# A Mamba image block: the next step's pieces at other units, and three products for GpSimd

## The chip, the cores and the metric

The kernel runs on one core of a Trainium2 chip. The metric is the device time of one execution in microseconds (us), lower is better. The engines are TensorE (PE, with its weight loads as PEld), VectorE (DVE), ScalarE (ACT), GpSimd (POOL) and SyncE (SP), which here issues every DMA. Each works off its own queue of instructions, and semaphores tie them together.

## The reference

The input is a batch of two images with 96 channels and 128 x 128 pixels. After a layer norm over the channels, four Mamba blocks each read the 16384 pixels as a sequence: by rows, by rows backward, by columns, by columns backward. The part in which the kernel spends most of its time is this (cut from the reference):

```python
xz = x @ in_w.T
xc, z = jnp.split(xz, 2, axis=-1)              # 192 inner channels each
xc = silu(causal_conv4(xc) + conv_b)           # depthwise, 4 taps
dt_raw, Bm, Cm = split(xc @ xproj_w.T)         # 6, 16 and 16 columns
dt = softplus(dt_raw @ dt_w.T + dt_b)
A = -jnp.exp(A_log)                            # 192 x 16
def step(h, t):                                # over the 16384 positions
    dA = jnp.exp(dt_t[:, :, None] * A)
    h = dA * h + dt_t[:, :, None] * B_t[:, None, :] * u_t[:, :, None]
    y = jnp.einsum('bds,bs->bd', h, C_t)
y = (y + Dp * xc) * silu(z)
return y @ outp_w.T
```

The four results are brought back to the order of the image, joined by a 1 x 1 product (`fuse_w`) and added to the input. Then come a feed-forward layer in a reduced float format, a 3 x 3 convolution and a second feed-forward layer, each with a norm ahead of it and a sum behind it.

## The kernel before

Each image goes through three stages: `normalize` (layer norm, and both orders of the pixels written to DRAM), `mamba`, and `ffn_and_conv`. Only `mamba` is touched by the change.

**Steps.** Two sequences are worked at once: first both forward ones, then both backward ones (`PAIRS`). Together they have 384 inner channels, which is three groups `g` of 128 partitions; group 0 belongs to the first sequence, group 2 to the second, group 1 is half and half. A step is 512 positions of both sequences. There are 32 steps for each pair, 64 per image, 128 in all.

**Units.** A step has 24 units (`nu`): group 0, 1 and 2 in turn, and for each the 16 states in pairs. Unit u is group u // 8, states 2 (u mod 8) and the next. Two units share a quad of four states, so a quad starts at every even unit. The step's own work, unit by unit, is:

- SP fetches a B tile and a C tile per quad from DRAM (`row_tile`, 128 x 4 x 512, 1 MB as written), B six units ahead of use and C four units ahead. There are four buffers for B and three for C. A fetch stands in SP's queue until the last reader of its buffer is done, and all later DMAs stand behind it.
- GpSimd multiplies a quad's B tile by dt times xc (`b_part`) and adds the state that enters the step to its first column (the fix, L347).
- ACT computes the decay exp(dt A) for the unit's two states into PSUM (`decay`, two units ahead), and copies the last column of each finished unit for the next step (`hst`, L446).
- VectorE runs one scan per state (`scan`, L357), and one product of both states with C (L445). For the units in `BY_POOL` the scan writes into the B tile in SBUF instead of the decay in PSUM, and GpSimd makes the product (`by_pool`, L364) a unit later.
- PE sums the products over the states in one PSUM bank y, by matmuls with the identity (`sums`, L361). A product by GpSimd is summed two units after its turn.
- At the first unit of a group VectorE multiplies the finished y by silu(z) (`gated`, L368), and PE opens the next y with D times xc (L452). After a group, `project` and `collect` add its share to the image.

**The loop.** Every engine's order is written out by hand (`in_order`), so what the loop issues first stands first in an engine's queue. One iteration k of it is:

```python
if k % 2 == 0:
    fetch(k + 2 * B_AHEAD, 0, B_AHEAD, bs)
    feed(k + AHEAD)                     # b_part
issue(k, 0)
... scan(0, ...); behind(k - 1); feed_decay(k + AHEAD); scan(1, ...)
if k % 2 == 0:
    fetch(k + 2 * C_AHEAD, 1, C_AHEAD, cs)
issue(k, 1)
```

`behind(k - 1)` holds the product, the hst copy and the sums of the unit before. `issue(k, where)` issues pieces that were put at that unit by `later`: where = 0 ahead of the scans, where = 1 at the end of the iteration.

**The next step's pieces.** While a step runs, the next one is prepared in pieces, whose units stand in a list in `prologue` as (unit, where, function). A unit from 24 on falls into the step itself, a negative one into the step before the one in which most of the pieces lie. The pieces are: `load` (two DMAs, tiles xa and xb), `conv` for each group (PE) with `conv_out` (ACT), `mix` (two DMAs that sort group 1's rows) and `silu` (ACT, with a table load before and one after); `rows` (PE: dt_raw, B and C of all positions), `rows_out` (ACT) and `rows_to_dram` (a DMA); `gate` (PE, the z half) with `gate_out` (ACT). For each group there is a chain for dt: `dt_in` (PE), `dt_exp` and `dt_ln` (three ACT instructions each), `dt_q`, `dt_log`, `dt_sum`, `dt_u` (GpSimd). `entry` (ACT) and `entering` (GpSimd) carry the state into the step. conv, rows, gate, dt_in and project all write to one PSUM tile, misc, which has a single buffer: each waits until ACT has read the one before.

Of the kernel before, what the change touches and what calls it, by code (L numbers as in the profile page):

```python
# [32 lines left out]
B_AHEAD = 3  # L33
C_AHEAD = 2
AHEAD = 2
BY_POOL = ((0, 4), (1, 4))
BCO = 32
NBC = 4 * S

# [2 lines left out]
def tile_metaformer(ctx: ExitStack, tc: tile.TileContext, a: dict, out: bass.AP):  # L42
# [136 lines left out]
    def mamba(acc, xnr, xnc):  # L179

        with ExitStack() as st:
# [25 lines left out]
            def prologue(pi, i, d):  # L207
# [107 lines left out]


                first = pi == 0 and i == 0
                at = [(-2, 1, load), (2, 1, partial(mix, "xc")), (6, 1, partial(silu, "xc"))]
                at += [(13, 1, partial(mix, "sz")), (28 if first else 22, 1, partial(silu, "sz"))]
                at += [(9, 0, rows), (10, 0, rows_out), (10, 1, rows_to_dram)]  # L320
                for g, k in ((1, 1), (0, 3), (2, 5)):
                    at += [(k, 0, partial(conv, g)), (k + 1, 0, partial(conv_out, g))]
                for g, k in ((1, 12), (0, 17), (2, 20)):
                    at += [(k, 0, partial(gate, g)), (k + 1, 0, partial(gate_out, g))]
                dts = ((24, 25, 26, 27), (31, 32, 33, 34)) if first else ((14, 15, 16, 18), (19, 20, 21, 23))
                for g, ks in enumerate(((10, 11, 12, 14), *dts)):
                    at += [(k, 0, partial(f, g)) for k, f in zip(ks, (dt_in, dt_exp, dt_ln, dt_q))]
                    at += [(ks[3] + m, 0, partial(f, g)) for m, f in ((1, dt_log), (1, dt_sum), (2, dt_u))]
                    if i > 0:
                        at += [((17, 23, 27)[g], 0, partial(entry, g)), (20 + 8 * g, 1, partial(entering, g))]  # L330

                outs = (conv_out, gate_out, rows_out, dt_exp)
                return sorted(at, key=lambda p: (p[0], p[1], getattr(p[2], "func", p[2]) not in outs))

            def row_tile(d, g, s, k, ahead):

# [19 lines left out]
            def scan(j, da, b, h):  # L356
                nc.vector.tensor_tensor_scan(h[:, j, :], da[:, j, :], b[:, j, :], 0.0, ALU.mult, ALU.add)  # L357

            def sums(s, y, c):
                for j in range(2):  # L360
                    nc.tensor.matmul(y, ident, c[:, j, :], start=False, stop=s + j == S - 1)  # L361
# [4 lines left out]
            def gated(pi, d, g, y):  # L366
                t = d["sz"][:, g, :]
                nc.vector.tensor_tensor(t, y, t, ALU.mult)  # L368
                d["yg"].append(t[:, ::-1] if pi == 1 else t)
# [17 lines left out]
            steps = [(pi, i) for pi in range(2) for i in range(NT)]  # L387
            units = [(g, s) for g in range(NG) for s in range(0, S, 2)]
            nu = len(units)
            total = nu * len(steps)  # L390
            state = [{} for _ in steps]
            todo = {}

            def later(k, where, f, *args):
                todo.setdefault((k, where), []).append(partial(f, *args))

            def issue(k, where):
                for f in todo.pop((k, where), ()):
                    f()

            for k, where, f in prologue(*steps[0], state[0]):
                if k < nu:
                    f()
                else:
                    later(k - nu, where, f)

            def prepare(n):
                if n < len(steps):
                    for m, where, f in prologue(*steps[n], state[n]):
                        k = (n - 1) * nu + m  # L410
                        if k < 0:
                            f()
                        else:
                            later(k, where, f)

            prepare(1)
            bs, cs, das, hs, quads = {}, {}, {}, {}, {}

            def fetch(k, n, ahead, m):
                if k < total:  # L420
                    t = row_tile(state[k // nu], *units[k % nu], n, ahead)
                    m[k], m[k + 1] = t[:, 0:2, :], t[:, 2:4, :]
                    if n == 0:
                        quads[k] = t

            def feed(k):

                if k < total:
                    n = k // nu
                    b_part(steps[n][1], state[n], *units[k % nu], quads.pop(k))  # L430

            def feed_decay(k):
                if k < total:
                    n = k // nu
                    das[k] = decay(steps[n][0], state[n], *units[k % nu])
# [3 lines left out]
            def behind(k):  # L439

                n, u = divmod(k, nu)
                (pi, i), d, (g, s) = steps[n], state[n], units[u]
                h, c = hs.pop(k), cs.pop(k)
                if (g, s) not in BY_POOL:
                    nc.vector.tensor_tensor(c, h, c, ALU.mult)  # L445
                nc.scalar.copy(hst[:, g, s : s + 2], h[:, :, T - 1])  # L446
                if s == 0:
                    if k > 0:
                        pn, pu = divmod(k - 1, nu)
                        gated(steps[pn][0], state[pn], units[pu][0], ys.pop(k - 1))  # L450
                    y = ps_y.tile([128, T], F32, name="y")
                    nc.tensor.matmul(y, dmat[:, pi, g, :], d["xc"][:, g, :], start=True, stop=False)  # L452
                else:
                    y = ys.pop(k - 1)
                ys[k] = y
                if (g, s) in BY_POOL:
                    later(k + 1, 1, by_pool, h, c)
                    later(k + 3, 1, sums, s, y, c)
                else:
                    sums(s, y, c)  # L460
                if k == total - 1:
                    gated(pi, d, g, y)
                if s == S - 2 and g > 0:
                    later(k + 3, 0, project, pi, i, d, g)
                    later(k + 3, 1, collect, pi, d, g)

            for m, (n, ahead) in ((bs, (0, B_AHEAD)), (cs, (1, C_AHEAD))):
                for k in range(ahead):
# [3 lines left out]
                feed_decay(k)  # L472
            for k in range(total + 6):
                n, u = divmod(k, nu)
                if u == nu - 2:

                    prepare(n + 2)
                if k % 2 == 0:
                    fetch(k + 2 * B_AHEAD, 0, B_AHEAD, bs)
                    feed(k + AHEAD)  # L480
                issue(k, 0)
                if k < total:
                    (g, s) = units[u]
                    da, b = das.pop(k), bs.pop(k)
                    hs[k] = b if (g, s) in BY_POOL else da
                    scan(0, da, b, hs[k])
                if 0 < k <= total:
                    behind(k - 1)
                feed_decay(k + AHEAD)
                if k < total:  # L490
                    scan(1, da, b, hs[k])
# [3 lines that stand above are left out]
# [102 lines left out]
    for b in range(NB):  # L597
        xnr = dpool.tile([C, L], F32, name="xnr")
        xnc = dpool.tile([C, L], F32, name="xnc")
        normalize(b, acc, xnr, xnc)  # L600
        mamba(acc, xnr, xnc)
        ffn_and_conv(b, acc)
# [71 lines left out]
```

## Time and profile before

| what | us |
|---|---|
| median of 3 runs | 12153.81 (12136.48 to 12159.19) |
| the profiled execution's own time | 12198.56 |
| its span, first to last instruction | 12196.8 |
| Mamba stage of the first image, 151.4 to 5532.9 | 5381.5 |
| Mamba stage of the second image, 6234.8 to 11618.2 | 5383.4 |
| VectorE busy in the first of these | 5177.9 |
| GpSimd busy in the first of these | 4869.7 |
| ACT busy in the first of these | 3888.1 |

The two Mamba stages are 88% of the span, so the time is mostly that of 128 steps. In the profile a group of instructions is a line of the kernel on one engine. Its row tells the busy time, the mean length of one instruction in ns, and after the bar the idle time of its engine just before it, with what ended most of that. An instruction's own length overlaps with its neighbour's a little on VectorE and ACT; where a chain is added up, the distance from one start to the next is the better measure. All B and C tiles carry the name row, the scan's result the name da, or row where it is written into the B tile.

### The profile page before, as it was taken

To read this page: it belongs to the slowest core of one execution; us is meant where nothing else is said; L and a number is where in the kernel's file an instruction comes from. 1 tells how busy PE (TensorE), PEld (TensorE's weight loads), DVE (VectorE), ACT (ScalarE), POOL (GpSimd) and SP (SyncE) were. 2 spreads that over 40 slices of the span, in tenths; PEclk is the share of its full clock that TensorE was granted. 3 is DMA by queue.
4 is the path that set the end of the run, shared out by engine and by line. 5 is a ranking of instruction groups with operands and counts; after the bars stand their busy time and mean duration, and the time that the engine had idled before them with its cause. 6 is when DMAs were issued, how large, how long until landed. Compare 5 with 4: busy or idle time off the path is not lost. (4 is left out here: it accounts for less than half of the span.)

```text
span 12196.8 us, 95712 instructions
## 1 busy us (share of the span) xinstructions
PE 10601.0 (87%) x24208; PEld 4012.8 (33%) x24208; DVE 10962.5 (90%) x10624; ACT 8585.5 (70%) x15110; POOL 9908.7 (81%) x5336
## 2 busy tenths in 40 slices
PE   7888888888888888888978888888888888888889
PEld 2333333333333333333323333333333333333333
DVE  6999999999999999995469999999999999999954
ACT  6777777777777777775577777777777777777655
POOL 5998999999998989891159989999989999988811
PEclk9999999999999999999989999999999999999999
DMA  7887888788877878781068888888878878878700
GB/s 250 309 319 302 307 319 313 309 318 312 318 310 306 319 305 310 308 317 47 26 242 307 308 317 312 314 318 313 313 307 308 321 308 316 314 305 309 304 32 13
DMA packets 539169, 3417.07 MB, mean 280 GB/s; under 512 B 67276, under 2 KB 68396, under 8 KB 140696
## 3 DMA queue, kind: packets, MB, share of 16 engines
q1 hardware_dynamic: 538616, 3410.94, 72.9%
q8 instruction: 195, 3.19, 0.1%
q14 instruction: 358, 2.93, 0.1%
HBM read 3289.04 MB, written 54.53 MB: 274 GB/s over the span
## 5 line engine op out<-in xcount | busy, mean ns | idle before, releaser
L345 POOL TENSOR_TENSOR row<-dtu,row 128x2048 f32<-128x2048 f32 x1536 | 6949.9, 4525 | 820.8 <-DMA row<-bcd 658.5
L357 DVE TENSOR_TENSOR_SCAN da<-da,row 128x512 f32<-128x512 f32 x5632 | 6650.2, 1215 | 509.8 <-ACT da L353 187.3
L361 PE MATMUL y<-row,ident 128*128 128x512 f32 x12288 | 5957.9, 618 | 1130.5 <-DVE row L445 1125.7
L353 ACT ACTIVATE da<-dt,amat 128x512 f32<-128x512 f32 x6144 | 4250.4, 692 | 278.7 <-DVE row L357 92.0
L361 PEld LDWEIGHTS y<-row,ident 128*128 128x128 f32 x12288 | 2268.5, 194 | 4643.0 <-issue 2296.4
L445 DVE TENSOR_TENSOR row<-da,row 128x1024 f32<-128x1024 f32 x2816 | 3395.8, 1206 | 1.0 <-DMA row<-bcd 0.9
L446 ACT COPY hst<-da 128x2 f32<-128x2 f32 x2816 | 434.7, 154 | 1423.8 <-DVE row L445 1412.4
L204 PE MATMUL misc<-xa,inx 96*64 96x512 f32 (+1 forms) x2048 | 963.6, 614 | 131.3 <-DMA xa<-xnr 108.0
L204 PE MATMUL misc<-xb,inx 96*64 96x512 f32 (+1 forms) x2048 | 962.3, 613 | 1.9 <-ACT xc L231 1.6
L568 POOL TENSOR_TENSOR acc<-acc,y 96x512 f32<-96x512 f32 x128 | 147.4, 1152 | 987.1 <-DVE y L567 987.1
L357 DVE TENSOR_TENSOR_SCAN row<-da,row 128x512 f32<-128x512 f32 x512 | 616.9, 1205 | 0.0
L364 POOL TENSOR_TENSOR row<-row,row 128x1024 f32<-128x1024 f32 x256 | 602.8, 2355 | 7.1 <-DVE row L357 6.1
L580 PE MATMUL pc<-pad,kw 96*96 96x512 f32 x1152 | 566.7, 593 | 0.0
L452 PE MATMUL y<-xc,dmat 128*128 128x512 f32 x768 | 428.9, 640 | 145.2 <-DVE sz L368 145.2
L295 POOL TENSOR_TENSOR q<-e,q 128x512 f32<-128x512 f32 x384 | 487.5, 1270 | 71.5 <-ACT q L292 71.5
L204 PEld LDWEIGHTS misc<-xa,inx 96*64 96x64 f32 (+1 forms) x2048 | 329.7, 166 | 650.6 <-issue 444.9
L231 ACT ACTIVATE xc<-misc,convb 128x512 f32<-128x512 f32 x256 | 175.8, 687 | 519.7 <-PE misc L204 519.7
L301 POOL TENSOR_TENSOR dt<-dt,ln 128x512 f32<-128x512 f32 x384 | 487.1, 1269 | 30.1
L298 POOL TENSOR_TENSOR ln<-ln,q 128x512 f32<-128x512 f32 x384 | 487.2, 1269 | 20.1
L305 POOL TENSOR_TENSOR dtu<-dt,xc 128x512 f32<-128x512 f32 x384 | 487.1, 1269 | 10.2
L378 PE MATMUL misc<-sz,gmat 128*96 128x512 f32 x1024 | 483.6, 594 | 0.0
L124 DVE TENSOR_TENSOR xq<-xm,rs 96x512 fp8e5<-96x512 f32 x128 | 87.9, 687 | 388.0 <-ACT rs L120 387.9
(81 smaller groups left out, 9340.4 us busy)
## 6 DMA issues: line engine op xcount, KB each, us to landing
row<-bcd SPq DMA_DIRECT2D x3072, 1024.0 KB, 7.1
xc<-mix SPq DMA_DIRECT2D x256, 128.0 KB, 5.3
sz<-mix SPq DMA_DIRECT2D x256, 128.0 KB, 5.4
xa<-xnr SPq DMA_DIRECT2D x124, 193.1 KB, 5.2
xb<-xnc SPq DMA_DIRECT2D x124, 193.1 KB, 5.5
bcd<-rows SPq DMA_DIRECT2D x128, 128.0 KB, 6.7
acc<-in_x_dram SPq DMA_DIRECT2D x16, 768.0 KB, 8.6
xnr<-xn SPq DMA_DIRECT2D x16, 768.0 KB, 4.3
```

The costliest lines, as they stand in the source:

```text
L204: nc.tensor.matmul(ps[rows, :], w(PAIRS[pi][d], k, lo, hi), src[d][:, k : k + T], **se)
L295: nc.gpsimd.tensor_tensor(d["q"], d["e"], d["q"], ALU.subtract)
L298: nc.gpsimd.tensor_tensor(d["ln"], d["ln"], d["q"], ALU.add)
L301: nc.gpsimd.tensor_tensor(d["dt"][g], d["dt"][g], d["ln"], ALU.add)
L305: nc.gpsimd.tensor_tensor(dtu, d["dt"][g], d["xc"][:, g, :], ALU.mult)
L345: nc.gpsimd.tensor_tensor(b, d["dtu"][g][:, None, :].broadcast_to((128, 4, T)), b, ALU.mult)
L353: nc.scalar.activation(da[:, j, :], d["dt"][g], AF.Exp, scale=amat[:, pi, g, s + j : s + j + 1])
L357: nc.vector.tensor_tensor_scan(h[:, j, :], da[:, j, :], b[:, j, :], 0.0, ALU.mult, ALU.add)
L361: nc.tensor.matmul(y, ident, c[:, j, :], start=False, stop=s + j == S - 1)
L364: nc.gpsimd.tensor_tensor(c, h, c, ALU.mult)
L445: nc.vector.tensor_tensor(c, h, c, ALU.mult)
L580: nc.tensor.matmul(pc, kw[:, t, :], rows, start=t == 0, stop=t == 8)
```

## The change

`BY_POOL` names three units instead of two: by their index in the step they are 4, 8 and 10, where they were 2 and 10. Most of the next step's pieces move to other units or to the other end of their iteration. `project` and `collect` move from three units after the group's end to four and five. Pieces at the same unit and place are now sorted by a rank, by which the ACT instructions that read misc come first, also against what `later` put there on its own.

| piece | before | after |
|---|---|---|
| load | 22, end | 21, end |
| conv of group 1, 0, 2 | 1, 3, 5 | 1, 5, 9 |
| conv_out | 2, 4, 6, ahead of the scans | 2, 6, 10, end |
| mix xc, silu xc | 2, 6, end | 3 ahead of the scans, 11 end |
| rows, rows_out, rows_to_dram | 9, 10, 10 end | 13, 14 end, 15 |
| gate of group 1, 0, 2 | 12, 17, 20 | 11, 18, 21 |
| gate_out | 13, 18, 21 | 12 end, 19, 22 |
| mix sz, silu sz | 13 end, 22 end | 13, 31 end (unit 7 of its own step) |
| dt_in, dt_exp, dt_ln, dt_q of group 0 | 10, 11, 12, 14 | 15, 16, 17, 17 end |
| of group 1 | 14, 15, 16, 18 | 17, 18, 20, 22 end |
| of group 2 | 19, 20, 21, 23 | 22, 23, 24, 26 end |
| entry of group 0, 1, 2 | 17, 23, 27 | 20, 25, 29 |
| entering, end | 20, 28, 36 | 21, 28, 36 |

```diff
-BY_POOL = ((0, 4), (1, 4))
+BY_POOL = ((0, 8), (1, 0), (1, 4))
...
-                at = [(-2, 1, load), (2, 1, partial(mix, "xc")), (6, 1, partial(silu, "xc"))]
-                at += [(13, 1, partial(mix, "sz")), (28 if first else 22, 1, partial(silu, "sz"))]
-                at += [(9, 0, rows), (10, 0, rows_out), (10, 1, rows_to_dram)]
-                for g, k in ((1, 1), (0, 3), (2, 5)):
-                    at += [(k, 0, partial(conv, g)), (k + 1, 0, partial(conv_out, g))]
-                for g, k in ((1, 12), (0, 17), (2, 20)):
-                    at += [(k, 0, partial(gate, g)), (k + 1, 0, partial(gate_out, g))]
-                dts = ((24, 25, 26, 27), (31, 32, 33, 34)) if first else ((14, 15, 16, 18), (19, 20, 21, 23))
-                for g, ks in enumerate(((10, 11, 12, 14), *dts)):
-                    at += [(k, 0, partial(f, g)) for k, f in zip(ks, (dt_in, dt_exp, dt_ln, dt_q))]
+                at = [(-3, 1, load), (3, 0, partial(mix, "xc")), (11, 1, partial(silu, "xc"))]
+                at += [(13, 0, partial(mix, "sz")), (31, 1, partial(silu, "sz"))]
+                at += [(13, 0, rows), (14, 1, rows_out), (15, 0, rows_to_dram)]
+                for g, k in ((1, 1), (0, 5), (2, 9)):
+                    at += [(k, 0, partial(conv, g)), (k + 1, 1, partial(conv_out, g))]
+                for g, k, out in ((1, 11, (12, 1)), (0, 18, (19, 0)), (2, 21, (22, 0))):
+                    at += [(k, 0, partial(gate, g)), (*out, partial(gate_out, g))]
+                dts = ((24, 25, 26, 27), (31, 32, 33, 34)) if first else ((17, 18, 20, 22), (22, 23, 24, 26))
+                for g, ks in enumerate(((15, 16, 17, 17), *dts)):
+                    at += [(k, 0, partial(f, g)) for k, f in zip(ks, (dt_in, dt_exp, dt_ln))]
+                    at += [(ks[3], 1, partial(dt_q, g))]
                     at += [(ks[3] + m, 0, partial(f, g)) for m, f in ((1, dt_log), (1, dt_sum), (2, dt_u))]
                     if i > 0:
-                        at += [((17, 23, 27)[g], 0, partial(entry, g)), (20 + 8 * g, 1, partial(entering, g))]
+                        at += [((20, 25, 29)[g], 0, partial(entry, g)), ((21, 28, 36)[g], 1, partial(entering, g))]
...
                 if s == S - 2 and g > 0:
-                    later(k + 3, 0, project, pi, i, d, g)
-                    later(k + 3, 1, collect, pi, d, g)
+                    later(k + 4, 0, True, project, pi, i, d, g)
+                    later(k + 5, 1, False, collect, pi, d, g)
...
-                if u == nu - 2:
+                if u == nu - 3:
```

More of the change, by code (lines that the diff above doesn't have):

```diff
@@ L328, in prologue @@
                     at += [(ks[3] + m, 0, partial(f, g)) for m, f in ((1, dt_log), (1, dt_sum), (2, dt_u))]
                     if i > 0:
-                        at += [((17, 23, 27)[g], 0, partial(entry, g)), (20 + 8 * g, 1, partial(entering, g))]
+                        at += [((20, 25, 29)[g], 0, partial(entry, g)), ((21, 28, 36)[g], 1, partial(entering, g))]
                 outs = (conv_out, gate_out, rows_out, dt_exp)
-                return sorted(at, key=lambda p: (p[0], p[1], getattr(p[2], "func", p[2]) not in outs))
+                at = [(k, where, getattr(f, "func", f) not in outs, f) for k, where, f in at]
@@ L335, in row_tile @@
+                return sorted(at, key=lambda p: p[:3])
             def row_tile(d, g, s, k, ahead):
@@ L392, in mamba, with later @@
             todo = {}
-            def later(k, where, f, *args):
-                todo.setdefault((k, where), []).append(partial(f, *args))
+            def later(k, where, rank, f, *args):
+                todo.setdefault((k, where), []).append((rank, partial(f, *args)))
             def issue(k, where):
-                for f in todo.pop((k, where), ()):
+                for _, f in sorted(todo.pop((k, where), ()), key=lambda p: p[0]):
                     f()
-            for k, where, f in prologue(*steps[0], state[0]):
+            for k, where, rank, f in prologue(*steps[0], state[0]):
                 if k < nu:
@@ L404, in mamba @@
                 else:
-                    later(k - nu, where, f)
+                    later(k - nu, where, rank, f)
             def prepare(n):
                 if n < len(steps):
-                    for m, where, f in prologue(*steps[n], state[n]):
+                    for m, where, rank, f in prologue(*steps[n], state[n]):
                         k = (n - 1) * nu + m
@@ L413, in prepare @@
                         else:
-                            later(k, where, f)
+                            later(k, where, rank, f)
             prepare(1)
@@ L456, in behind @@
                 if (g, s) in BY_POOL:
-                    later(k + 1, 1, by_pool, h, c)
-                    later(k + 3, 1, sums, s, y, c)
+                    later(k + 1, 1, True, by_pool, h, c)
+                    later(k + 3, 1, True, sums, s, y, c)
                 else:
```

## The prediction

> **What bounds the kernel now.** I read the page first: engine totals, then the costliest groups (a row ends with busy us, mean ns of one | idle before it and what ended it).
>
> ```profile
> PE 10601.0 (87%) x24208; PEld 4012.8 (33%) x24208; DVE 10962.5 (90%) x10624; ACT 8585.5 (70%) x15110; POOL 9908.7 (81%) x5336
> ...
> L345 POOL TENSOR_TENSOR row<-dtu,row 128x2048 f32<-128x2048 f32 x1536 | 6949.9, 4525 | 820.8 <-DMA row<-bcd 658.5 <-DVE sz L368 152.5 <-ACT da L353 5.7
> L357 DVE TENSOR_TENSOR_SCAN da<-da,row 128x512 f32<-128x512 f32 x5632 | 6650.2, 1215 | 509.8 <-ACT da L353 187.3 <-ACT hst L446 157.8 <-POOL row L345 103.3
> L445 DVE TENSOR_TENSOR row<-da,row 128x1024 f32<-128x1024 f32 x2816 | 3395.8, 1206 | 1.0 <-DMA row<-bcd 0.9
> L364 POOL TENSOR_TENSOR row<-row,row 128x1024 f32<-128x1024 f32 x256 | 602.8, 2355 | 7.1 <-DVE row L357 6.1
> ```
>
> VectorE looks like the bound and GpSimd like the spare engine. Then the windows: one image's Mamba stage, a common step, a bad step (columns: PE, PEld, DVE, ACT, POOL busy, clock, DMA share, GB/s).
>
> ```profile
> 151.40:5532.90 5381.50, 4688.50 (x10557) 1770.15 (x10554) 5177.93 (x4670) 3888.08 (x6879) 4869.73 (x2591) 0.98 0.81 311
> ...
> 1834.33:1917.46 83.13, 73.42 (x168) 27.57 (x167) 80.85 (x74) 61.19 (x109) 76.32 (x42) 0.98 0.83 317
> 2333.13:2422.80 89.67, 77.31 (x168) 28.75 (x167) 80.97 (x74) 60.97 (x109) 76.40 (x42) 0.94 0.77 294
> ```
>
> A common step takes 83.13 us. The first takes 80.8, so the other 63 average (5381.5 - 80.8) / 63 = 84.14. The bad steps have the same VectorE work; the waits of PE charge them to the input tile (xa for conv: 108.0 us over the run, 33 times, the start's 28.4 among them).
>
> Third, the timelines of the common step: one row of DVE, two of POOL, then PE, then SP.
>
> ```profile
> 1855.96 1.23 DVE L357 TENSOR_TENSOR_SCAN da<-da,row 128x512 f32<-128x512 f32 x1 [1.23 <-ACT hst L446]
> ```
>
> ```profile
> 1870.07 4.52 POOL L345 TENSOR_TENSOR row<-dtu,row 128x2048 f32<-128x2048 f32 x1 [4.90 <-DMA row<-bcd]
> ...
> 1874.82 2.35 POOL L364 TENSOR_TENSOR row<-row,row 128x1024 f32<-128x1024 f32 x1
> ```
>
> ```profile
> 1878.87 7.33 PE L361 MATMUL y<-row,ident 128*128 128x512 f32 x12 [1.85 <-DVE row L445]
> ```
>
> ```profile
> 1886.23 0.33 SPq L341 DMA_DIRECT2D row<-bcd  x1
> 1886.61 1.14 SPq L248 DMA_DIRECT2D sz<-mix  x2
> 1887.85 0.53 SPq L341 DMA_DIRECT2D row<-bcd  x1
> ```
>
> I write scan(u) for the first scan of unit u, b(u) for the B product of the quad that starts there. Here scan(4) is at 1847.88 and scan(6) at 1855.96. At 1870.07 POOL waits for b(12)'s tile; from there it never rests until it has fed scan(4) of the next step, at 1931.05, which waits 0.43 us for it. So 14.11 us (scan(6), SP's queue, landing, b(12)) + 60.98 (POOL) + 8.08 (scan(4) to scan(6)) = 83.17: **the step is a loop through four queues**, no one engine. The PE row ends with the sums of unit 10, which GpSimd multiplied; the C tile in unit 10's buffer is issued at once (1886.23), and b(20)'s tile 1.6 us later, behind it in SP's queue.
>
> [...] SP waits 5435.7 us in all for y's matmuls. [...] b with its fix 4.75 us, a dt operation 1.35 (1.23 ahead of b), a product 2.32 (1874.82 to 1877.14). [...] VectorE's product reads da, which is in PSUM, and its 1.12 us from start to start beside POOL shows no slowing.
>
> **The change, part by part.** *The product.* VectorE has 21 instead of 22 per step. A unit without one takes 2.38 us (1874.11 to 1876.49) instead of 3.36, so 0.98 is saved, 125 us over 128 steps if VectorE were the bound; its work is 80.85 - 0.98 = 79.9. POOL's work is 83.13 less its waits (4.90 + 0.51) = 77.7, and becomes 80.0. Neither exceeds the step: both could run at 80.0.
>
> *Conv at 1, 5, 9, conv_out behind the decays.* This thins PE's crowd at units 1 to 6, on which ACT waits: VectorE's waits of 1.23 and 0.59 us on ACT go. *Load at 21 for 22*: the two DMAs (0.42 us each on SP) go out one quad earlier, past SP's B and C fetches of unit 22; the xa waits, 84.14 - 83.13 = 1.0 per step, go. These two edits alone open the old loop by 1.2 + 1.0 us.
>
> *Product units 4, 8, 10 for 2 and 10.* Sums of a GpSimd unit come two units after their turn in PE's queue, and SP cannot fetch the C tile that reuses the buffer before they end; all later fetches queue behind it. At unit 2 this fell into the conv crowd (the C tile for unit 8 went out at 1862.26, 14.4 us after scan(4)); at 4 it does not. By my working below, unit 4's sums end at t = 2.6 and unit 8's at 14, their C tiles (units 10 and 14) go out there, and b(14)'s and b(18)'s tiles, next on SP, land at about 13.5 and 23 with POOL wanting them at 14.1 and 23.8: hidden, by 0.6 us in the tighter case.
>
> *Project one, collect two units later, the order by rank, prepare at nu - 3*: taken as nothing; PE and ACT have room there (ACT is busy 61.2 of 83.1). *mix xc one unit later in SP's queue*: hidden by the silu, which comes 8 units after it. *rows_to_dram* at 15 (was 10): its landing (median 6.7 us, two units) ends before SP fetches from it at 18.
>
> *Gate, rows and dt of group 0.* Gate g1's copy is at 12, rows at 13 (was 9), dt_in, dt_exp, dt_ln of group 0 at 15, 16, 17 (was 10 to 12), and the silu of xc, 4.09 us with its two table loads, at 11 (was 6). **Here a new wait arises**: misc has one buffer, so rows stands in PE's queue, ahead of unit 12's sums, until gate_out. With t = 0 at scan(8), durations from the trace, start to start:
> - VectorE: units 8 to 11 take 3.36, 2.84 (no product, one gate), 3.36, 2.38; with 0.2 of waiting, scan(12) is at 12.1, scan(14) 18.9, scan(17) 29.0.
> - ACT: unit 9's product ends 8.7; hst and decay 1.54, conv_out 0.59: 10.9; hst, decay 1.6: 12.5; silu 4.1: 16.6; hst, decay 1.5: 18.1; gate_out 0.6: 18.7.
> - PE: rows start 19.1 [...], six matmuls of 0.43: 21.7. Behind it the sums of 12, 10, 13, each 1.72: unit 10's end 25.3, dt_in 28.0. Without rows ahead, unit 12's could have started at 17.9.
> - ACT: dt_exp 1.7: 29.7; hst, decay 1.5: 31.2; dt_ln 2.1: 33.3. POOL, which after b(14) at 18.9 had only b(16) and b(18) (4.75 each) and rests since 28.5, starts dt_q, after 1.23 b(20): **34.6**.
> - SP: unit 16's C tile 25.4, mix sz twice, b(20)'s tile 27.0; landing 7.0 (1887.85 to 1894.85): 34.0. Nearly as late.
> - POOL from b(20) to the end of b(8): 7 x 4.75 + 3.9 (rest of group 0) + 10.3 (groups 1, 2) + 0.4 + 2.3 = 50.2. So the next scan(8) is at 34.6 + 50.2 + 0.05 = **84.8**.
>
> VectorE's and POOL's savings end as waits: POOL idles 4.8 us ahead of dt_q, VectorE some 4 us for b(6) and b(8).
>
> The sum: (84.8 - 84.14) x 126 steps = +83 us. The profiled execution would go from its own 12198.56 to 12282. It is 0.4% over the median of the runs, 12153.81; I put the same 83 us there: 12237.
>
> **Unknown costs.** The order at unit 13 is not in the trace. If rows waits for nothing, dt_ln ends 2.6 us after scan(17), POOL needs 51.4 us from dt_q to b(8), and VectorE 28.8 to scan(17): 2.7 + 51.4 + 28.9 = 83.0. If b(20)'s tile lands as slowly as one of this step did (10.3 us), it is 37.3 + 50.2 = 87.5 at worst. I take the chain above: every link has a measured duration.
>
> **Rivals.**
> - *The waits go and nothing replaces them* (faster). dt_in is done before ACT reaches dt_exp at unit 16 (0.55 us after scan(16), 26.2 on the scale above) and b(20)'s tile has landed by 33: 83.0 per step, 1.14 x 126 = -144: 12010. For it: the old loop is opened, and SP's long stall around unit 4 goes. Against: rows would have to be off PE's path by 2 us. It decides from where dt_in ends: each us earlier than 28.0 takes a us off the step, down to 83.0, since unit 10's sums, and with them the tile, move with it. Chance 0.28.
> - *POOL as the bound*: 80.0 per step, -4.1 x 126 = -520: 11633. It needs POOL never to wait for dt_ln, which comes just a unit ahead of dt_q. Chance 0.05.
> - *A wash*: the new loop at 84.14, 12154. Chance 0.10.
> - *A second wait on top*: unit 16's C tile lands after VectorE wants it, or ACT waits at unit 23 for dt_q of group 1, which now follows b(24), so that decays come late: up to 1 us more, 85.8, 12363. Chance 0.12; the forecast itself 0.45.
>
> **How the numbers follow.** About 0.2% is what a measurement can tell from no change. Slower 0.45 + 0.12 = 0.57, same 0.10, faster 0.33. The range runs from just below the first rival, 11990, to near the last, 12350; the forecast alone holds 12170 to 12310.
>
> **What would show it.** In the changed profile: POOL's L364 rows (now L366) x384; its idle time moved from DMA row<-bcd before b(12) to ACT q before dt_q, or the tile of b(20); VectorE waiting for POOL row at units 6 and 8; hardly a PE wait for xa; steps of one length near 84.8. Steps near 83 with dt_in ahead of ACT would prove my chain wrong; steps near 80, the whole reading.

## The result, and the profile after

| | before | after |
|---|---|---|
| median, us | 12148.27 of 4 runs (12136.48 to 12159.19) | 12342.83 of 4 runs (12336.99 to 12347.67) |
| profiled execution, its own time | 12198.56 | 12347.67 |
| a step's mean length in it, from scan(8) to scan(8) | 84.2 | 85.4 |

The ratio is **1.016, 95% interval 1.0143 to 1.0178**: slower by 194.6 us, where +83 was forecast. (The profiled executions differ by 149.1 us; the rest is told below.) The sign and the chain behind it were right, the size was not.

The page of the changed kernel first: the engine totals, and of its costliest groups those that answer to the rows shown of before (busy us, mean ns of one | idle before it and what ended it).

```profile
PE 10619.9 (86%) x24208; PEld 3936.3 (32%) x24208; DVE 10835.2 (88%) x10496; ACT 8548.2 (69%) x15110; POOL 10204.7 (83%) x5464
...
L347 POOL TENSOR_TENSOR row<-dtu,row 128x2048 f32<-128x2048 f32 x1536 | 6952.4, 4527 | 7.9 <-DMA row<-bcd 7.5
L359 DVE TENSOR_TENSOR_SCAN da<-da,row 128x512 f32<-128x512 f32 x5376 | 6353.7, 1215 | 420.5 <-POOL row L349 295.1
...
L447 DVE TENSOR_TENSOR row<-da,row 128x1024 f32<-128x1024 f32 x2688 | 3242.8, 1206 | 161.1 <-DMA row<-bcd 156.8
...
L359 DVE TENSOR_TENSOR_SCAN row<-da,row 128x512 f32<-128x512 f32 x768 | 929.1, 1210 | 205.9 <-POOL row L349 200.4
L295 POOL TENSOR_TENSOR q<-e,q 128x512 f32<-128x512 f32 x384 | 487.8, 1270 | 745.9 <-ACT hst L448 663.7
...
L366 POOL TENSOR_TENSOR row<-row,row 128x1024 f32<-128x1024 f32 x384 | 904.4, 2355 | 0.4 <-issue 0.4
L258 PE MATMUL misc<-xc,bcw 128*96 128x512 f32 x768 | 489.2, 789 | 278.6 <-ACT hst L448 202.0
```

GpSimd's 820.8 us of waiting ahead of b is now 7.9, and 745.9 us of waiting ahead of dt_q (L295, 71.5 before) have come in its place. VectorE waited for ACT at units 6 and 9; now it waits for GpSimd's B products, at units 6 and 8. 156.8 us ahead of L447 are nearly all the C tile of unit 16, which lands late. The last row did not matter in the profile of before: rows (L258), 354.8 us and 598 ns there, now costs 789 ns a matmul.

The windows show why (columns as before; PEclk is the third number from the end): one image's Mamba stage, two steps that follow each other, then rows alone in each of these kinds of step.

```profile
149.50:5606.70 5457.20, 4697.11 (x10563) 1731.91 (x10560) 5114.64 (x4606) 3868.99 (x6879) 5017.72 (x2655) 0.99 0.80 307
...
1852.30:1936.60 84.30, 72.58 (x166) 26.84 (x166) 79.92 (x73) 60.78 (x108) 78.56 (x43) 1.00 0.82 312
1936.60:2022.70 86.10, 74.32 (x166) 27.34 (x166) 79.97 (x73) 60.85 (x108) 78.67 (x44) 0.98 0.80 307
1902.50:1905.20 2.70, 2.60 (x6) 1.09 (x7) 2.62 (x3) 1.48 (x4) 2.62 (x4) 1.00 0.70 294
1986.90:1991.20 4.30, 4.25 (x6) 1.57 (x7) 4.20 (x5) 2.83 (x6) 4.22 (x4) 0.60 0.45 189
```

VectorE's work is 79.9 in both steps, as forecast, but there are **two lengths of step, 84.4 and 86.1 us**. The same six matmuls ran once at the full clock (a granted 1.00), once at a granted 0.60. The timelines at these two places (start, length; in brackets the idle time before), with ACT's copy of the gate, gate_out (L239), ahead of the first:

```profile
1901.96 0.58 ACT L239 COPY mix<-misc 128x512 f32<-128x512 f32 x1
...
1902.60 2.82 PE L258 MATMUL misc<-xc,bcw 128*96 128x512 f32 x6 [2.14 <-DMA row<-bcd]
1905.25 3.17 PE L363 MATMUL y<-row,ident 128*128 128x512 f32 x7
...
1986.95 4.51 PE L258 MATMUL misc<-xc,bcw 128*96 128x512 f32 x6 [2.15 <-DMA row<-bcd]
1991.30 3.17 PE L363 MATMUL y<-row,ident 128*128 128x512 f32 x7
```

Rows stands waiting for gate_out: its first matmul starts 0.06 us after that copy ends at 1902.54 (the DMA in the brackets is not what it waits for). PE idles 2.14 us, and the burst that follows runs at half clock (a granted 0.50) for most of its length in 75 of the 128 steps. The next sums start 2.65 or 4.35 us after rows does, and the whole chain behind them moves by these 1.7 us. Here it is in the shorter step, from the C tile for unit 16 over dt_in, dt_exp and dt_ln to dt_q; scan(8) is at 1884.13:

```profile
1908.88 0.33 SPq L343 DMA_DIRECT2D row<-bcd  x1
...
1910.49 1.12 PE L276 MATMUL misc<-rows,dtw 12*128 12x512 f32 x2
...
1911.65 0.69 ACT L281 ACTIVATE e<-misc,dtb 128x512 f32<-128x512 f32 x1 [1.30 <-PE misc L276]
...
1916.17 0.72 ACT L292 ACTIVATE q<-q,minus_one 128x512 f32<-128x512 f32 x1
...
1916.97 1.27 POOL L295 TENSOR_TENSOR q<-e,q 128x512 f32<-128x512 f32 x1 [4.33 <-ACT hst L448]
```

ACT waits for dt_in, GpSimd for dt_ln (its last instruction, L292, ends at 1916.89; the hst copy named in the brackets stands right behind it on ACT). dt_q starts at 1916.97 - 1884.13 = 32.84 and the next scan(8) comes at 84.36. In the longer step it is 34.54 and 86.08: both times 51.5 from dt_q to the end.

### The profile page after: what moved, and what is told of

It is laid out like the page before. It is cut to its first block, busy times and chain, and to the rows that moved or that the text cites. A ratio compares the mean times of both kernels' runs of the same rounds, so it can differ in the third digit from the quotient of the medians.

```text
span 12345.9 us, 96110 instructions
## 1 busy us (share of the span) xinstructions
PE 10619.9 (86%) x24208; PEld 3936.3 (32%) x24208; DVE 10835.2 (88%) x10496; ACT 8548.2 (69%) x15110; POOL 10204.7 (83%) x5464
## 5 line engine op out<-in xcount | busy, mean ns | idle before, releaser
L359 DVE TENSOR_TENSOR_SCAN da<-da,row 128x512 f32<-128x512 f32 x5376 | 6353.7, 1215 | 420.5 <-POOL row L349 295.1
L363 PE MATMUL y<-row,ident 128*128 128x512 f32 x12288 | 5800.9, 606 | 967.1 <-DVE row L447 965.7
L363 PEld LDWEIGHTS y<-row,ident 128*128 128x128 f32 x12288 | 2231.1, 190 | 4396.9 <-issue 2188.6
L447 DVE TENSOR_TENSOR row<-da,row 128x1024 f32<-128x1024 f32 x2688 | 3242.8, 1206 | 161.1 <-DMA row<-bcd 156.8
L359 DVE TENSOR_TENSOR_SCAN row<-da,row 128x512 f32<-128x512 f32 x768 | 929.1, 1210 | 205.9 <-POOL row L349 200.4
L295 POOL TENSOR_TENSOR q<-e,q 128x512 f32<-128x512 f32 x384 | 487.8, 1270 | 745.9 <-ACT hst L448 663.7
L366 POOL TENSOR_TENSOR row<-row,row 128x1024 f32<-128x1024 f32 x384 | 904.4, 2355 | 0.4 <-issue 0.4
L258 PE MATMUL misc<-xc,bcw 128*96 128x512 f32 x768 | 489.2, 789 | 278.6 <-ACT hst L448 202.0
L281 ACT ACTIVATE e<-misc,dtb 128x512 f32<-128x512 f32 x384 | 261.5, 681 | 557.2 <-PE misc L276 287.3
```

Of the source, the lines that this page charges most:

```text
L258: nc.tensor.matmul(d["ps"][0 : BCO + NBC, :], bcw[:, pi, g, :], d["xc"][:, g, :], start=g == 0, stop=g == NG - 1)
L295: nc.gpsimd.tensor_tensor(d["q"], d["e"], d["q"], ALU.subtract)
L366: nc.gpsimd.tensor_tensor(c, h, c, ALU.mult)
```

## The experiments

My theory after the result: the step is the chain scan(8), gate's copy, rows, sums of 12, 10 and 13, dt_in, dt_ln, dt_q, and from there 51.5 us of GpSimd; half clock in rows makes part of the steps longer. The rivals: the third product overloads GpSimd; the late tile closes the loop. Ratios are to the kernel before, run beside on the same chip, with 95% intervals.

**Third product alone.** The kernel before with one line changed (which also moves unit 2's product to unit 4):

```diff
-BY_POOL = ((0, 4), (1, 4))
+BY_POOL = ((0, 8), (1, 0), (1, 4))
```

> The kernel before with the new product units 4, 8, 10 alone; every piece stays where it was. The theory (rows, put between the sums of units 11 and 12 in PE's queue, waits for gate_out and makes dt_in and the sums of unit 10 late) has no such wait here: rows stays at unit 9. GpSimd's work is 80.0 us a step, below the 83.7 that the unprofiled runs of before give, so the time is that of before or less, 0.985 to 1.003, and GpSimd shows no wait of several us for dt_ln. The rival, that the third product itself is what costs the time, expects most of the slowing here: 1.010 to 1.018.

Measured: 12169.73, ratio 1.0022 (1.0014 to 1.003). Steps are 83.6, some longer. GpSimd is not overloaded, for it still waits, and nothing is gained either. The page of this run:

```profile
L357 DVE TENSOR_TENSOR_SCAN da<-da,row 128x512 f32<-128x512 f32 x5376 | 6330.4, 1214 | 598.8 <-ACT da L353 466.4
...
L364 POOL TENSOR_TENSOR row<-row,row 128x1024 f32<-128x1024 f32 x384 | 902.5, 2350 | 455.8 <-DVE row L357 291.9
```

VectorE now waits for ACT's decays (units 5 and 9), GpSimd for the scans whose products it makes. In this order of pieces the saved VectorE work turns into waits.

**The moved pieces alone.** The changed kernel with the old line `BY_POOL = ((0, 4), (1, 4))`.

> The changed kernel with the old product units 2 and 10: the moved pieces alone. The theory keeps its chain (the silu at 11, gate_out at 12, rows at 13, unit 10's sums behind rows, dt_q of group 0 at 17), while GpSimd has 2.3 us less to do between b(20) and b(8), all of it on the loop (it is unit 4's product that goes from this stretch, unit 2's that comes, so nothing is gained there; only unit 8's, off the loop, is gone). So the step stays near 85.3 us: 1.012 to 1.020. The rival that blames the third product expects the time of before, 0.995 to 1.003.

Measured: 12528.78, ratio 1.0322 (1.0305 to 1.0339): slower as the theory said, but by twice as much. Steps are 86.0 and 87.7. Two things add up. The product of unit 8 is back on VectorE between scan(8) and the gate, so gate_out of group 1 ends 1.1 us later (18.94 to 19.52, for 17.84 to 18.41), and dt_q comes at 33.95 for 32.84. And unit 2's product stands ahead of b(6) in GpSimd's queue, where unit 4's stood behind it, so scan(6) waits 3.9 us for GpSimd, for 1.65 in the changed kernel, and units 6 and 7 on VectorE, 6.75 us, still lie between it and scan(8): the part from dt_q on takes 52.1 for 51.5. GpSimd also waits 2.0 us per step ahead of unit 10's product, with unit 8's gone; that wait lies before dt_q and lengthens nothing. I had priced the product by VectorE's whole step, in which it was slack; by its place on the loop, **unit 8's product is worth 1.1 us per step**.

**The gate's copy one unit earlier, at the end of unit 11 and so ahead of the silu.** The changed kernel with:

```diff
-                for g, k, out in ((1, 11, (12, 1)), (0, 18, (19, 0)), (2, 21, (22, 0))):
+                for g, k, out in ((1, 11, (11, 1)), (0, 18, (19, 0)), (2, 21, (22, 0))):
```

> The changed kernel with the one instruction gate_out of group 1 moved from the end of unit 12 to the end of unit 11, where it stands ahead of the silu of xc. rows then waits for the silu alone, 2.4 us earlier (about 16.0 us after scan(8) instead of 18.5). The theory expects the sums of unit 10 and dt_in some 2.4 us earlier, GpSimd's wait for dt_ln shorter by 1.2 to 3, no rows at half clock, and steps of 83.0 to 83.4 us: 0.990 to 0.997. A rival for which the length of the step comes from GpSimd's load or from elsewhere expects no change: 1.014 to 1.018.

Measured: 12059.02, ratio 0.9935 (0.9918 to 0.9951), steps of 83.1. gate_out ends at 12.7 for 18.4, PE no longer stands, the C tile for unit 16 goes out at 22.4 and VectorE does not wait for it, dt_q starts at 31.64. One place in ACT's queue turns the change from a loss of 1.6% into a gain of 0.65%. Rows is back at 599 ns a matmul. dt_q on the page of this run:

```profile
L295 POOL TENSOR_TENSOR q<-e,q 128x512 f32<-128x512 f32 x384 | 486.9, 1268 | 469.4 <-ACT hst L448 387.4
```

Its wait is down from 745.9 to 469.4 us, 3.1 per step: dt_q still closes the loop, only earlier.

**PE kept busy, the chain left as it is.** The changed kernel with two matmuls with zero weights ahead of rows, which add nothing to y and fill the wait (the trace has two records for each such matmul, so four):

```diff
+            zero = one.tile([C, 128], F32, name="zero")
+            nc.vector.memset(zero, 0.0)
...
+                    for _ in range(2):
+                        nc.tensor.matmul(now["y"], zero, inx[:, 0].rearrange("c k w -> c (k w)")[:, 0:T], start=False, stop=False)
...
-                at += [(13, 0, rows), (14, 1, rows_out), (15, 0, rows_to_dram)]
+                at += [(13, 0, warm), (13, 0, rows), (14, 1, rows_out), (15, 0, rows_to_dram)]
```

> The changed kernel with two matmuls of zero weights, added into y just ahead of rows, which fill PE's 2.1 us of idling there and change no value; nothing else moves. If the two lengths of its steps (84.4 and 86.0 us) come from rows running at half clock after that idling, rows takes 2.6 us in every step and the steps are nearly all 84.4: 1.004 to 1.008. If the long steps come from elsewhere (a C tile late, DMA), the two lengths remain: 1.014 to 1.018.

Measured: 12215.43, ratio 1.0064 (1.0044 to 1.0084). Of the 126 steps 116 are within 0.2 of 84.3; the second common length is gone. PE's timeline of this run (rows is L267):

```profile
1877.88 1.88 PE L214 MATMUL y<-inx,zero 96*128 96x512 f32 x4
1880.19 2.82 PE L267 MATMUL misc<-xc,bcw 128*96 128x512 f32 x6 [0.43 <-DMA row<-bcd]
```

With 1.88 us of work put into the idle time, rows takes 2.82, and 611 ns a matmul over the whole run, for 789. Of the 194.6 us, 12342.83 - 12215.43 = 127 are the half clock, which is 75 steps of 1.7 us.

**The load edit alone.** The kernel before with `load` at -3 for -2 and `prepare` at nu - 3.

> The kernel before with its load one unit earlier (and the preparation of the step after next one unit earlier, so that the load can be placed there), nothing else. If the irregular steps of the kernel before come from the input tile landing late (waits for xa), its steps become all of the common length, 83.1 us against a mean of 84.1 to 84.2: at most 1.0 x 126 = 126 us off the profiled run and some 50 to 80 us off the others, ratio 0.990 to 0.997; that would put the load edit of the changed kernel at a gain. Rival: the irregular steps have another cause, or the earlier load only moves SP's other fetches: 0.998 to 1.004.

Measured: 12078.21 (12077.98 to 12079.92), ratio 0.9943 (0.9927 to 0.996). Nearly all steps are 83.1. So the irregular steps of before are the late input tile; they cost 12198.56 - 12079.92 = 119 us in the profiled execution of before, and 12146.85 - 12078.21 = 69 in the others. The runs of before beside it lie between 12114.58 and 12160.52, those of this kernel within 2 us: what varied in before was that wait.

**Rows a unit later in PE's queue.** The changed kernel with `(14, 0, rows)` for `(13, 0, rows)`, behind the sums of 12 and 10; gate and silu stay late.

> The changed kernel with rows one unit later in PE's queue, behind the sums of units 12 and 10 of its turn; gate and silu stay where they are. Theory (the wait for gate_out in PE's queue delays unit 10's sums, the C tile for 16 and dt_in): PE no longer idles ahead of rows, rows takes about 2.2 us in every step, sums of unit 10 end at about 21 to 22 after scan(8), VectorE has no wait for a C tile at unit 17, dt_in at 25.5 to 26.5, b(20) at about 33: steps of 83.2 to 83.8, ratio to the kernel before 0.993 to 1.001. Rival (the order in PE's queue does not matter, the loop is closed by GpSimd's third product and the later dt): the steps stay at 84.3 or more, 1.006 to 1.018.

Measured: 12118.68, ratio 0.9982 (0.9973 to 0.9991), steps of 83.6. gate_out still ends at 18.4, but nothing on the loop stands behind it: the C tile for 16 goes out at 21.4, dt_in at 25.6, dt_q at 32.10. The place of rows in PE's queue decides, not what GpSimd has to do.

**dt a unit earlier too.** The run with the gate's copy earlier (at the end of unit 11; the expectation below says its start), and:

```diff
-                at += [(13, 0, rows), (14, 1, rows_out), (15, 0, rows_to_dram)]
+                at += [(13, 0, rows), (13, 1, rows_out), (14, 0, rows_to_dram)]
...
-                for g, ks in enumerate(((15, 16, 17, 17), *dts)):
+                for g, ks in enumerate(((14, 15, 16, 16), *dts)):
```

> The changed kernel with the gate's copy at the start of unit 11 (as in the run with gate_out earlier, whose steps took 83.1), and also the dt chain of group 0 one unit earlier (14, 15, 16, 16) and the two row copies a unit earlier. Theory: in that run GpSimd still rested 3.1 us ahead of dt_q, which opened its chain; with dt_q a unit earlier only the tile of b(20), landing about 31.2 after scan(8), closes the loop: steps of about 81.5, ratio 0.975 to 0.983. Rival: GpSimd's own order or another wait on ACT holds the step, and most of the 3.1 us comes back as a wait elsewhere: 0.988 to 0.996.

Measured: **11708.23 (11701.99 to 11710.27), ratio 0.9638 (0.9624 to 0.9652)**, steps of 80.3: faster than the range expected, and the fastest of all. The tile that I took for the next bound is not one. dt_q starts at 28.75, and the rest of group 0's dt now runs ahead of b(20), which starts at 32.66, when its tile has been there since 31.05. The list of GpSimd's groups:

```profile
L347 POOL TENSOR_TENSOR row<-dtu,row 128x2048 f32<-128x2048 f32 x1536 | 6955.1, 4528 | 4.3 <-DMA row<-bcd 3.9
L366 POOL TENSOR_TENSOR row<-row,row 128x1024 f32<-128x1024 f32 x384 | 904.0, 2354 | 1.1 <-DVE row L359 0.7 <-issue 0.4
...
L295 POOL TENSOR_TENSOR q<-e,q 128x512 f32<-128x512 f32 x384 | 487.2, 1269 | 108.0 <-ACT q L292 78.0 <-ACT hst L448 29.9
```

GpSimd waits ahead of b, the product and dt_q are down to 4.3, 1.1 and 108.0 us. Of the last, 78.0 came in two waits outside the common steps; the other 122 waits share 29.9, some 0.25 each. **GpSimd is the bound**, at the 80.0 of work that the prediction added up.

**Sums of GpSimd's units one unit earlier too**, `later(k + 2, ...)` for `later(k + 3, ...)` with sums.

> As the run with the dt chain earlier, and also the sums of GpSimd's units one unit earlier in PE's queue, so that their C tiles, and the B tiles queued behind them on SP, go out earlier. Theory (the landing of b(20)'s tile closes the loop): the steps come down towards GpSimd's own work, 80.0 to 80.4 by the sum of its instructions: 80.4 to 81.5, ratio 0.962 to 0.978. Rival: PE now waits for GpSimd's products and ACT's decays come late behind it: 0.98 to 1.00.

Measured: 11756.22, ratio 0.9679 (0.9664 to 0.9693): in the range given, but 48 us slower than without it, so the theory that the tile's landing still mattered falls. The sums of unit 8 now stand ahead of the gate on PE, gate_out starts at 13.35 for 12.12, ACT is late and VectorE waits 0.97 for it at unit 14, dt_q moves from 28.75 to 29.15 and the step from 80.3 to 80.7.

**Two products in the good order.** The fastest kernel with `BY_POOL = ((0, 8), (1, 4))`. The expectation below misnames the units: it is unit 8's product that goes back to VectorE, and GpSimd keeps those of 4 and 10.

> As the run with gate_out and the dt chain earlier (its steps took 80.26), but GpSimd makes two units' products, 8 and 20, for three; VectorE makes unit 2's again. If the third product pays where GpSimd never waits: GpSimd's work is 77.7, VectorE's 80.85 and its short waits, so VectorE closes the loop: steps of 80.9 to 81.3, 0.6 to 1.0 us more, ratio 0.969 to 0.975. Rival (the step is held by something that both share, and the third product is worth nothing here either): 80.2 to 80.4, ratio 0.963 to 0.966.

Measured: 11950.06, ratio 0.9838 (0.9823 to 0.9853): a miss, by more than the theory and far from the rival. Steps are 81.4 and 82.9. I had priced VectorE's work again, not the place: dt_q comes at 29.88 for 28.75, the same 1.1 us as above. The second length is the half clock at another place, the sums ahead of rows (a granted 0.54 on the mean of 2323.20 to 2326.70). PE's timeline of a common and of a longer step:

```profile
2241.88 1.98 PE L363 MATMUL y<-row,ident 128*128 128x512 f32 x4 [2.34 <-DVE row L447]
...
2323.26 3.54 PE L363 MATMUL y<-row,ident 128*128 128x512 f32 x4 [2.34 <-DVE row L447]
```

So the third product, worth nothing on its own, is worth 11950.06 - 11708.23 = 242 us in the good order. In the profiled executions it is 211.5: 1.1 us in 126 steps, 142 in all, and some 66 for the half clock in 43 longer steps.

**dt earlier, the gate's copy left late.** The changed kernel with the two edits of the dt run alone.

> The changed kernel with the dt chain of group 0 one unit earlier and the two row copies with it, while the gate's copy stays at the end of unit 12, so that rows still waits. Theory (the step is dt_q's start + 51.5, dt_q being 6.5 after dt_in, dt_in behind rows and the sums of 12 and 10 but now ahead of those of 13): dt_in at 24.6, dt_q at 31.1, steps of 82.6 where rows takes 2.2 us and 84.3 where it takes 3.9, mean near 83.6, ratio 0.990 to 1.002. Rival (b(20)'s tile, landing 33.6 or 35.3 in the changed kernel, closes the loop, or ACT, whose row copy now stands right behind rows, brings decays late): 84.3 to 86 per step, 1.006 to 1.018.

Measured: 12072.94, ratio 0.9943 (0.9927 to 0.996). dt_in at 24.64, dt_q at 31.12, steps of 82.6; where rows runs long, dt_q at 32.82 and 84.3. Each as expected; the tile that lands at about 35 in the longer steps does not close the loop.

All kernels with the changed kernel's pieces, times after scan(8), of common steps; two values where there are two lengths:

| kernel | dt_q starts | step | from dt_q on |
|---|---|---|---|
| after | 32.84, 34.54 | 84.36, 86.08 | 51.5 |
| moved pieces alone | 33.95, 35.64 | 86.01, 87.72 | 52.1 |
| gate's copy earlier | 31.64 | 83.12 | 51.5 |
| PE kept busy | 32.85 | 84.31 | 51.5 |
| rows later | 32.10 | 83.57 | 51.5 |
| dt earlier, copy late | 31.12, 32.82 | 82.59, 84.31 | 51.5 |
| two products | 29.88, 31.42 | 81.38, 82.91 | 51.5 |
| sums earlier | 29.15 | 80.66 | 51.5 |
| gate's copy and dt earlier | 28.75 | 80.26 | 51.5 |

The step is dt_q's start plus 51.5 in every one with three products or with two of units 4 and 10. That is the loop, shown by moving dt_q's start over nearly 6 us, from 28.75 to 34.54.

## Why the prediction was right in kind and wrong in size

**Right.** The old loop opened: the waits ahead of b fell from 820.8 (658.5 of it for tiles) to 7.9, the waits of VectorE on ACT went. The new wait was where it was put, rows behind gate_out in PE's queue, and the links came in the forecast order: gate_out 18.41 (18.7 forecast), dt_in 26.36 at its start, 27.5 at its end (28.0), dt_q 32.84 (33.4), then 51.5 to the end (51.4). The waits turned up as named: GpSimd 5.3 us ahead of dt_q (4.8), VectorE 1.6 each at units 6 and 8 (some 4 in all). Without the half clock the step is 84.36, for 84.8: rows starts at 18.47 for 19.1, since gate_out ends 0.3 earlier and rows follows it by 0.06 us, where the forecast left 0.4 between them.

**The step that failed: "rows start 19.1 ..., six matmuls of 0.43: 21.7".** The 0.43 is the spacing in the trace of before (rows at 1867.22, at a granted 1.00). In 75 of 128 steps the burst ran at half clock (0.50), and the sums of unit 12 started at 22.82 for 21.12. The forecast had made the condition for it itself, a PE that stands still until gate_out, and priced only the standing. What it cost was measured by filling the idle time: 127 us. The warning lay in a row that the prediction printed: 12 matmuls of sums at 1878.87 took 7.33 us after 1.85 us of idling. A window over its first part, in the trace of before:

```profile
1878.80:1883.00 4.20, 4.06 (x5) 1.47 (x6) 4.20 (x5) 3.64 (x8) 4.12 (x4) 0.59 1.02 393
```

The clock was 0.59 on the mean of this window; the second to the fourth sum start 0.86 and 0.85 apart, for 0.43. There, in this step, it cost nothing: the fifth waits for VectorE's next product and starts 3.37 us after the first, which is a unit's 3.36. I read the row as the wait in its brackets and not as its length.

**The second that failed: "I put the same 83 us there".** The base of 84.14 per step holds about 1.0 us of waits for xa, and these are larger in the profiled execution of before (119 us) than in its other runs (69). The changed kernel has none outside the start of a sequence, so its runs lie 5 below its profile (12342.83 and 12347.67) while those of before lie 50 below theirs. A change that removes an irregular wait must be carried over from the step without it.

The terms: +83 forecast; (84.36 - 84.8) x 126 = -55, since the chain was 0.44 shorter; +127 half clock; +50 base of before; -5 for the changed kernel's own profile: 200, where 194.6 was measured. That the chain came out shorter was luck: it took off what would have made the miss larger.

**The rivals.** *The waits go and nothing replaces them*, 83.0: it names its condition rightly, rows off PE's path, and the runs that meet it have 83.1 and 83.6. *POOL as the bound*, 80.0: reached at 80.3 by the run with dt a unit earlier, again by the condition named. *A second wait on top*: unit 16's C tile was late, by 1.2 us at unit 17, as it said; but that wait is not on the loop, since dt_q follows dt_in and not VectorE. Its 12363 is near the result for another reason, the half clock. *A wash* did not occur.

## What to carry to other kernels

Where a step is a loop through several queues, move its latest link and watch the step follow; an engine's saved work is worth what its place on that loop makes it worth (nothing, or 1.1 us for one product), not its share of the busy time. If a piece stands in PE's queue ahead of work that others wait for, have its releaser done earlier or put the piece behind that work; one unit's difference was worth 2.3% here (1.016 to 0.9935). And when PE is made to wait, price the matmuls behind the wait at half clock as well (here a granted 0.50, which cost 1.7 us in 75 of 128 steps), and take the base from steps without irregular waits.

## What the hardware showed that was not expected

In these traces the length of the idle time ahead of a burst of matmuls does not tell whether it runs at half clock: rows waits 2.14 and 2.15 us in the two steps above. The granted clock is either 1.00 or 0.50 throughout the traces of before and after, and all its changes in each of them (209 and 195) lie within 1 ns of marks that stand 3413.3 ns apart. Here are intervals between such marks in the changed kernel (columns as before): the one that holds most or all of the wait ahead of rows and the next one, in the shorter step, then the same two and one more in the longer step.

```profile
1898.75:1902.17 3.42, 1.70 (x4) 0.39 (x3) 3.42 (x4) 3.33 (x6) 3.42 (x1) 1.00 0.86 343
1902.17:1905.58 3.41, 2.98 (x7) 1.28 (x8) 3.33 (x4) 1.98 (x6) 3.33 (x4) 1.00 0.64 271
...
1984.09:1987.50 3.41, 1.26 (x4) 0.28 (x3) 3.31 (x4) 3.30 (x7) 3.33 (x4) 1.00 0.99 399
1987.50:1990.92 3.42, 3.42 (x6) 1.15 (x5) 3.42 (x4) 1.98 (x5) 3.42 (x2) 0.50 0.39 161
1990.92:1994.33 3.41, 3.41 (x10) 1.50 (x9) 3.41 (x4) 2.17 (x5) 3.33 (x3) 1.00 0.02 5
```

The wait is the same, but in the shorter step one of the marks splits it: PE worked 1.70 us of the interval, and the clock stayed at 1.00. In the longer step PE worked 1.26 us, 37%, and the next whole interval ran at 0.50. That loses 3.41 / 2 = 1.7 us of matmuls, the difference between the two lengths of step. All 75 slow bursts of rows have an interval ahead of them in which PE was busy for at most 40.7%; in the intervals ahead of the 53 others it was at least 41.3%. So in this kernel the slow steps are told by where the wait lies between the marks, not by how long it is.

This holds for rows alone, and no share of busy time sorts every interval: in the Mamba stages of before the clock stayed at 1.00 after one with PE busy for 40.9%, and went to 0.50 after one with 52.1%. Nor does the idle time there: after 1.15 to 1.65 us of it none of 540 bursts begins slowly (two starts more than 0.8 us apart among the first four matmuls), but after 0.8 to 1.0 us 10 of 25 do. What decides it was not shown.
